# The end of the last feed-forward: roots cut into pieces, statistics from accumulators, norms and stores on ScalarE

## Chip, cores and metric

One core of one Trainium2 chip runs the whole program. The time is device time of one execution in microseconds (us), and less is better. A core has five engines with queues of their own, each in order: TensorE (PE, with its weight loads PEld), VectorE (DVE), ScalarE (ACT), GpSimd (POOL) and SyncE (SP), which here only issues DMAs. An instruction that waits holds up everything behind it on its engine.

## What is computed

A decoder of two layers with six sub-blocks (called A to F in the kernel), each followed by a layer norm of the residual sum. The activations are 4 batches of 512 rows by 512 columns, float32. The change touches the last sub-block only, a feed-forward with 4-bit weights, an RMS norm and the layer norm behind it:

```
def _L1_ffn_ref(x, gate_up_packed, gate_up_scales, down_packed, down_scales):
    ...
    gate_up = jnp.einsum('bsh,oh->bso', x, w_gu)
    gate, up = (gate_up[..., :I], gate_up[..., I:])      # I = 1408
    h = jax.nn.silu(gate) * up
    y = jnp.einsum('bsi,hi->bsh', h, w_down)
    rms = jnp.sqrt(jnp.mean(y * y, axis=-1, keepdims=True) + EPS)
    return y / rms
...
x = _layernorm(x + _L1_ffn_ref(x, ...), axis=-1)
```

with `_layernorm(x) = (x - mean) / sqrt(var + 1e-5)` over the 512 columns of a row.

## The kernel before

Every sub-block is a Python generator for one batch. `lanes` steps two of them in turn, so that the end of one batch is traced between the pieces of the next. The order of tasks is `E3 F0 F1 F2 F3` at the end, and a task may start when the one before it has said `"next"`. The framework's scheduler then orders the traced instructions on each engine and places the buffers and all waits; the order in the built program is therefore not quite the order of the source. `tc.issue_after(ins)` ties the instructions of a block behind `ins` on the engine of `ins`, as an order of issue alone.

`l1_ffn(b)` is F for batch `b`. It loads four tiles x of 128 rows by 512 and transposes them (`fx`, split into the pair `fxh`, `fxl`). Then it goes over 11 blocks of 128 hidden columns, each with `u` = 0 (gate) and 1 (up), and each of these over four groups `g` of 128 inputs, since every group has a scale of its own. One such piece is two matmuls into a PSUM bank `fg` (L1063), and `scaled` empties the bank: ScalarE writes g = 0 with its scale (L1021) and the gate's g = 3 into another tile (L1024), GpSimd adds that one (L1031), and VectorE adds the others to the running sum (L1027, called a scaled sum below; five of them in a block). Later follow Silu on ScalarE (L1035), the product on VectorE (L1039), the split into `fhh` on ScalarE (L1044) and `fhl` on GpSimd (L1045), and twelve matmuls into the four accumulators `facc` of the batch (L1054). A pass of the block has 28 matmuls: 16 of the pieces and 12 of the accumulators.

PSUM has eight banks in one pool. Four are held by the accumulators of a batch until its end. A next batch's pieces turn in the four that are left until its own accumulators start, so a bank that is freed late stops TensorE, whose queue is in order.

The end of a batch, called its tail, begins behind `yield "next"`: the residual x is loaded a second time; ScalarE squares the four accumulators with row sums (`fsq`, L1073); VectorE turns the sums into a mean square (L1076) and takes the inverse root for four columns at once: a shift (L158), a seed (L159), and three Newton steps of three operations (L161, L162, L163), all on 128x4. Then VectorE forms x + y/rms from PSUM (L1080), collects row statistics (`bn_stats` L168, `bn_aggr` L169), takes the second inverse root (L177, L158 to L163), and normalizes (L186). SP stores the four tiles (L189). The tails of F0, F1 and F2 lie beside the pieces of the next batch; the tail of F3 has nothing beside it.

```
        ss, ve = fm[:, 0:4], fm[:, 4:8]
        for i in range(NT):
            sq = self.t("fsq")
            nc.scalar.activation(sq, acc[i], AF.Square, accum_out=ss[:, i : i + 1])
```

Of the kernel before, what the change touches and what calls it, by code (L numbers as in the profile page):

```python
# [14 lines left out]
I32 = mybir.dt.int32  # L15
U8 = mybir.dt.uint8
AF = mybir.ActivationFunctionType
ALU = mybir.AluOpType
# [4 lines left out]
P = 128  # L23
NT = 4
MAGIC = 12582912.0
RSQRT_SEED = float(0x5F3759DF)
# [38 lines left out]
class Net:  # L65
# [88 lines left out]
    def rsqrt(self, ve, s):  # L154

        nc = self.nc
        sh, y, t = s[:, 0:4], s[:, 4:8], s[:, 8:12]
        nc.vector.tensor_scalar(sh.bitcast(I32), ve.bitcast(I32), 1, None, ALU.logical_shift_right)  # L158
        nc.vector.tensor_scalar(y.bitcast(I32), sh.bitcast(I32), -1.0, RSQRT_SEED, ALU.mult, ALU.add)  # L159
        for _ in range(3):  # L160
            nc.vector.tensor_tensor(t, y, y, ALU.mult)  # L161
            nc.vector.scalar_tensor_tensor(t, t, -0.5, ve, ALU.mult, ALU.mult)  # L162
            nc.vector.scalar_tensor_tensor(y, t, 1.5, y, ALU.add, ALU.mult)  # L163
        return y

    def ln_stats(self, y, i, ln):
        nc = self.nc
        nc.vector.bn_stats(ln[:, 8:14], y)  # L168
        nc.vector.bn_aggr(ln[:, 2 * i : 2 * i + 2], ln[:, 8:14])  # L169
# [835 lines left out]
    def l1_ffn(self, b):  # L1005
        nc = self.nc
        pipe = Pipe()
        x = self.load_x(5, b)
        yield
        yield  # L1010
        xT = []
        yield from self.feature_major(pipe, x, "fx", xT)
        yield from pipe.drain()
        acc, y, hs = [], {}, {}

        def scaled(i, u, g, ps):

            s = self.gs[:, (i * 2 + u) * 4 + g : (i * 2 + u) * 4 + g + 1]
            if g == 0:
                y[u] = self.t("fg")  # L1020
                nc.scalar.activation(y[u], ps, AF.Copy, scale=s)  # L1021
            elif g == 3 and u == 0:
                y2 = self.t("fg2")
                nc.scalar.activation(y2, ps, AF.Copy, scale=s)  # L1024
                y[u, 2] = y2
            else:
                nc.vector.scalar_tensor_tensor(y[u], ps, s, y[u], ALU.mult, ALU.add)  # L1027
            if g == 3:
                o = y.pop(u)
                if (u, 2) in y:  # L1030
                    nc.gpsimd.tensor_tensor(o, o, y.pop((u, 2)), ALU.add)  # L1031
                pipe.later(F_ACT, *((up, i, o) if u else (gate, o)))

        def gate(o):
            nc.scalar.activation(o, o, AF.Silu)  # L1035
            y["gate"] = o

        def up(i, o):
            nc.vector.tensor_tensor(o, o, y.pop("gate"), ALU.mult)  # L1039
            pipe.later(F_PAIR, pair, i, o)  # L1040

        def pair(i, o):
            hi, lo = self.t("fhh", F32R), self.t("fhl", F32R)
            nc.scalar.copy(hi, o)  # L1044
            nc.gpsimd.tensor_tensor(lo, o, hi.bitcast(F32), ALU.subtract)  # L1045
            for t in range(NT):
                pipe.later(F_DOWN + 2 * t, down, i, t, (hi, lo))

        def down(i, t, h):
            if len(acc) <= t:  # L1050
                acc.append(self.pb("facc"))
            c = slice(t * P, (t + 1) * P)
            for n, (l, r) in enumerate(((0, 0), (0, 1), (1, 0))):
                nc.tensor.matmul(acc[t], h[l][:, c], self.dn[i][r], start=i == 0 and n == 0, stop=i == 10 and n == 2)  # L1054

        for i in range(11):
            self.need("F", lambda: len(self.dn) > min(10, i + 1))
            for u in range(2):
                for g in range(4):
                    pipe.tick()  # L1060
                    ps = self.pa("fg")
                    for n in range(2):
                        nc.tensor.matmul(ps, self.gu[i, u][:, g * P : (g + 1) * P], xT[g][n], start=n == 0, stop=n == 1)  # L1063
                    pipe.later(F_SCALED, scaled, i, u, g, ps)
                    yield
        yield "next"
        x = self.load_x(5, b)
        yield from pipe.drain()
        fm = self.s("fm", 24, 2)
# [4 lines that stand above are left out]
            if i % 2:  # L1074
                yield
        nc.vector.tensor_scalar(ve, ss, 1.0 / 512.0, 1e-6, ALU.mult, ALU.add)  # L1076
        r = self.rsqrt(ve, fm[:, 8:20])
        ln = self.ln_tile()
        for i in range(NT):
            nc.vector.scalar_tensor_tensor(x[i], acc[i], r[:, i : i + 1], x[i], ALU.mult, ALU.add)  # L1080
            self.ln_stats(x[i], i, ln)
            if i % 2:
                yield
        self.finish(pipe, x, ln, 5, b)
        yield from pipe.drain()

    def need(self, key, ready):

# [119 lines left out]
```

## Time and profile before

| | |
|---|---|
| three runs | 1684.18, 1685.69 (median), 1687.63 us |
| the profiled execution | 1684.66 us, span 1682.9 us from its first to its last instruction |
| mean granted TensorE clock | 0.974 |
| TensorE busy | 1557.8 us, 93% of the span |
| VectorE busy | 1286.9 us, 76% |
| ScalarE busy | 1005.9 us, 60% |
| GpSimd busy | 675.3 us, 40% |
| scaled sums on VectorE (L1027) | 220, 162.3 us, 745 ns each |
| norms of all layer norms on VectorE (L186) | 96, 57.1 us |
| statistics of all layer norms on VectorE (L168) | 96, 66.0 us, 688 ns each |
| squares on ScalarE (L1073) | 16, 9.4 us, and 16 reads of the accumulator, 3.2 us |

In a timeline line the columns are the start, the duration, the engine, the line of the source, the operation, what it writes and reads with shapes, and how many of them follow each other; brackets hold the idle time before it and who ended it. In a line of the windows view the stretch is followed by its length, then busy time (and instructions) of PE, PEld, DVE, ACT and POOL, the granted clock, the DMA engines' busy share and GB/s. "L1027" is line 1027 of the kernel. The change inserts lines ahead of these, so that the scaled sum L1027 is L1043 in the changed kernel, the product L1039 is L1055, and the squares L1073 are L1089.

### The profile page before, as it was taken

Reading aid. Unit: us, or ns where it says so; the run is one execution under the profiler, and the core shown is the slowest. Engines: PE = TensorE matmul, PEld = TensorE weight load, DVE = VectorE, ACT = ScalarE, POOL = GpSimd, SP = SyncE. Lnnn points to the kernel's source line nnn. Section 1 sums busy time; section 2 is a strip of 40 time slices with the busy share of each in tenths; the row PEclk is TensorE's granted clock in tenths of the full one; section 3 lists DMA queues with packets and bytes.
Section 4 is the critical chain, followed back from the end, with each engine's and each line's share of the span. In section 5 each row is a group of like instructions: output and inputs, shape, how many; then the busy total and the mean of one; then the engine's idle time right before and its main releaser. Section 6 shows DMA issues by size and latency. Waiting matters only on the chain.

```text
span 1682.9 us, 25852 instructions
## 1 busy us (share of the span) xinstructions
PE 1557.8 (93%) x8246; PEld 1110.3 (66%) x8246; DVE 1286.9 (76%) x2804; ACT 1005.9 (60%) x2145; POOL 675.3 (40%) x672
## 2 busy tenths in 40 slices
PE   6899899999999989998999999999997889999995
PEld 4678687444454665466777767777676766786874
DVE  5787657999976668886565675756888999979795
ACT  4233243789877876876596864968624444444542
POOL 5574562555535401530344323353324345333332
PEclk8899999999999989999999999999999999999998
DMA  8572441454313742664441322423434632020000
GB/s 274 175 233 74 118 107 63 151 159 146 97 51 141 219 116 89 207 205 107 141 111 42 84 77 78 124 67 86 142 111 143 211 96 72 1 76 33 19 26 25
DMA packets 108359, 189.18 MB, mean 112 GB/s; under 512 B 17584, under 2 KB 19632, under 8 KB 108224
## 3 DMA queue, kind: packets, MB, share of 16 engines
q1 hardware_dynamic: 104096, 179.08, 34.9%
q0 software_dynamic: 4128, 8.46, 2.0%
q8 instruction: 65, 1.06, 0.3%
q14 instruction: 70, 0.57, 0.1%
HBM read 111.98 MB, written 41.94 MB: 91 GB/s over the span
## 4 chain that ended last, share of the span: by engine, by line
PE 49%; DVE 25%; ACT 9%; DMA 8%; issue 5%; POOL 2%; SPq 1%; DVEq 0%; ACTq 0%; POOLq 0%
PE fg L1063 6%; PE facc L1054 5%; DVE bsm L399 3%; PE dT L841 3%; DMA z<-had_scratch 2%; DVE fg L1027 2%; ACT de L831 2%; PE do L861 2%; PE pu L611 2%; DVE x L186 2%; PE dn L663 2%; PE pg L609 2%; PE dq L146 2%; PE dq L147 2%; PE dq L148 2%
## 5 line engine op out<-in xcount | busy, mean ns | idle before, releaser
L1027 DVE SCALAR_TENSOR_TENSOR fg<-fg,gs,fg 128x512 f32<-128x512 f32 x220 | 162.3, 745 | 36.8 <-PE fg L1063 17.8
L1063 PE MATMUL fg<-fxh,gu 128*128 128x512 f32 x352 | 144.0, 409 | 7.6 <-DVE fg L1027 4.6
L831 ACT ACTIVATE de<-de,dm 128x128 f32<-128x128 f32 (+3 forms) x256 | 143.0, 563 | 13.3 <-DVE dm L830 12.4
L830 DVE CUSTOM_DVE_ANT_0 de<-ds,negm,thr 128x128 f32<-128x128 f32 (+3 forms) x256 | 126.6, 546 | 31.1 <-PE ds L819 28.0
L407 POOL TENSOR_SCALAR be<-be,bsm 128x512 f32<-128x512 f32 x128 | 96.3, 765 | 117.1 <-DVE bsm L405 73.6
L1063 PE MATMUL fg<-fxl,gu 128*128 128x512 f32 x352 | 139.0, 395 | 0.0
L588 POOL TENSOR_TENSOR hl<-g,hh 128x512 fp32r<-128x512 f32 x64 | 84.0, 1320 | 115.7 <-ACT hh L587 96.1
L1031 POOL TENSOR_TENSOR fg<-fg,fg 128x512 f32<-128x512 f32 x44 | 61.1, 1388 | 128.5 <-ACT fg L1024 89.5
L401 ACT ACTIVATE be<-bs,bsm 128x512 f32<-128x512 f32 x128 | 87.6, 691 | 36.2 <-DVE bsm L399 30.3
L761 POOL TENSOR_TENSOR dql<-dqf,dqh 128x512 fp32r<-128x512 f32 x32 | 41.4, 1295 | 154.4 <-ACT dqh L760 120.8
L841 PE MATMUL dT<-ident,de 128*128 128x128 f32 x640 | 90.6, 279 | 7.9 <-ACT de L831 5.9
L1063 PEld LDWEIGHTS fg<-fxh,gu 128*128 128x128 f32 x352 | 66.9, 190 | 38.1 <-DVE fg L1027 14.3
L841 PEld LDWEIGHTS dT<-ident,de 128*128 128x128 f32 x640 | 72.2, 142 | 26.5 <-ACT de L831 13.4
L1021 ACT ACTIVATE fg<-fg,gs 128x512 f32<-128x512 f32 x88 | 60.4, 686 | 39.4 <-PE fg L1063 39.0
L399 DVE TENSOR_REDUCE bsm<-bs 128x1 f32<-128x512 f32 x128 | 83.9, 673 | 0.0
L677 PE MATMUL had<-had,z 128*128 128x128 f32 x512 | 74.2, 290 | 10.4 <-DMA z<-had_scratch 9.3
L1054 PE MATMUL facc<-p4h,fhh 128*128 128x512 f32 x176 | 71.6, 408 | 9.0 <-DVE fg L1027 6.2
L677 PEld LDWEIGHTS had<-had,z 128*128 128x128 f32 x512 | 68.0, 201 | 17.8 <-DMA z<-had_scratch 7.2
L423 PE MATMUL bo<-bpT,cT 128*64 128x512 f32 x256 | 75.7, 618 | 2.6 <-ACT bpT L414 1.5
L199 PEld LDWEIGHTS bT<-ident,be 128*128 128x128 f32 x512 | 54.8, 141 | 34.9 <-issue 11.8
L199 PE MATMUL bT<-ident,be 128*128 128x128 f32 x512 | 73.1, 281 | 4.7 <-POOL be L407 2.5
L135 ACT CAST qkh<-z 128x512 fp32r<-128x512 f32 x32 | 19.6, 620 | 94.4 <-POOL z L291 86.3
(329 smaller groups left out, 4759.8 us busy)
## 6 DMA issues: line engine op xcount, KB each, us to landing
x<-x SPq DMA_DIRECT2D x176, 256.0 KB, 3.1
had_scratch<-hw SPq DMA_DIRECT2D x64, 256.0 KB, 2.0
z<-had_scratch SPq DMA_DIRECT2D x64, 256.0 KB, 6.8
stk<-dqh SPq DMA_DIRECT2D x192, 64.0 KB, 2.0
tw<-in_wg_t SPq DMA_DIRECT2D x32, 256.0 KB, 4.5
sw<-z SPq DMA_DIRECT2D x64, 128.0 KB, 2.4
tw<-in_wu_t SPq DMA_DIRECT2D x32, 256.0 KB, 3.7
tw<-in_wd_t SPq DMA_DIRECT2D x32, 256.0 KB, 3.3
```

What stands on the lines that cost most here:

```text
L199: self.nc.tensor.transpose(pt[:, i * P : (i + 1) * P], srcs[i][:, j * P : (j + 1) * P], self.ident)
L399: nc.vector.tensor_reduce(sm[:, h : h + 1], ps, AX.X, ALU.max, negate=True)
L401: nc.scalar.activation(e, ps, AF.Exp, bias=sm[:, h : h + 1], accum_out=sm[:, 2 + h : 3 + h])
L407: nc.gpsimd.tensor_scalar(es[h][i], es[h][i], sm[:, 4 + h : 5 + h], 1.0, ALU.mult, ALU.mult)
L588: nc.gpsimd.tensor_tensor(lo, g, hi.bitcast(F32), ALU.subtract)
L677: nc.tensor.matmul(ps[:, c * P : (c + 1) * P], z[g * 4 + c][:, i * P : (i + 1) * P], self.had16, start=True, stop=True)
L830: nc.vector.tensor_tensor_reduce(es[i], ps, self.negm[:, 384 - P * i :], -1.0, self.thr[:, i : i + 1], ALU.add, ALU.min, n4[:, i : i + 1])
L831: nc.scalar.activation(es[i], es[i], AF.Exp, bias=n4[:, i : i + 1], scale=-1.0, accum_out=den[:, hh * 4 + i : hh * 4 + i + 1])
L841: nc.tensor.transpose(pt[:, o + (i - j) * P : o + (i - j + 1) * P], es[i][:, j * P : (j + 1) * P], self.ident)
L1027: nc.vector.scalar_tensor_tensor(y[u], ps, s, y[u], ALU.mult, ALU.add)
L1054: nc.tensor.matmul(acc[t], h[l][:, c], self.dn[i][r], start=i == 0 and n == 0, stop=i == 10 and n == 2)
L1063: nc.tensor.matmul(ps, self.gu[i, u][:, g * P : (g + 1) * P], xT[g][n], start=n == 0, stop=n == 1)
```

## The change

The inverse root can be issued in pieces: `rsqrt_spread` is a generator that issues shift and seed, and after a `yield` each one Newton step, every piece tied behind the scaled sum that was traced last (`self.summed`). Both roots of the tail use it. The row sums of the residual come from `accum_out` of the operation that forms it; GpSimd turns each into a negative mean; ScalarE squares x minus the mean with row sums. The norm becomes one ScalarE activation with a scale and a bias column, the bias from one GpSimd product, and ScalarE issues the stores. `finish`, which the other sub-blocks still use, is no longer called here.

```diff
+    def rsqrt_spread(self, ve, s):
+
+        nc = self.nc
+        sh, y, t = s[:, 0:4], s[:, 4:8], s[:, 8:12]
+        with self.tc.issue_after(self.summed.ins):
+            nc.vector.tensor_scalar(sh.bitcast(I32), ve.bitcast(I32), 1, None, ALU.logical_shift_right)
+            nc.vector.tensor_scalar(y.bitcast(I32), sh.bitcast(I32), -1.0, RSQRT_SEED, ALU.mult, ALU.add)
+        for _ in range(3):
+            yield
+            with self.tc.issue_after(self.summed.ins):
+                self.newton(ve, y, t)
...
-                nc.vector.scalar_tensor_tensor(y[u], ps, s, y[u], ALU.mult, ALU.add)
+                self.summed = nc.vector.scalar_tensor_tensor(y[u], ps, s, y[u], ALU.mult, ALU.add)
...
         nc.vector.tensor_scalar(ve, ss, 1.0 / 512.0, 1e-6, ALU.mult, ALU.add)
-        r = self.rsqrt(ve, fm[:, 8:20])
+        yield from self.rsqrt_spread(ve, fm[:, 8:20])
+        r = fm[:, 12:16]
         ln = self.ln_tile()
-        for i in range(NT):
-            nc.vector.scalar_tensor_tensor(x[i], acc[i], r[:, i : i + 1], x[i], ALU.mult, ALU.add)
-            self.ln_stats(x[i], i, ln)
+        tot, nmean, sq, nr = (ln[:, 4 * n : 4 * n + 4] for n in range(4))
+        for i in range(NT):
+
+            nc.vector.scalar_tensor_tensor(x[i], acc[i], r[:, i : i + 1], x[i], ALU.mult, ALU.add, accum_out=tot[:, i : i + 1])
+            nc.gpsimd.tensor_scalar(nmean[:, i : i + 1], tot[:, i : i + 1], -1.0 / 512.0, 1.0, ALU.mult, ALU.mult)
+            t = self.t("fsq")
+            nc.scalar.activation(t, x[i], AF.Square, bias=nmean[:, i : i + 1], accum_out=sq[:, i : i + 1])
             if i % 2:
                 yield
-        self.finish(pipe, x, ln, 5, b)
-        yield from pipe.drain()
+        v2 = ln[:, 16:20]
+        nc.vector.tensor_scalar(v2, sq, 1.0 / 512.0, 1e-5, ALU.mult, ALU.add)
+        yield from self.rsqrt_spread(v2, ln[:, 20:32])
+        r2 = ln[:, 24:28]
+        nc.gpsimd.tensor_tensor(nr, nmean, r2, ALU.mult)
+        yield
+        for i in range(NT):
+            nc.scalar.activation(x[i], x[i], AF.Identity, bias=nr[:, i : i + 1], scale=r2[:, i : i + 1])
+            nc.scalar.dma_start(self.xd[6][b, i * P : (i + 1) * P, :], x[i])
+            yield
```

In the changed kernel the residual is L1099, the means L1100, the squares L1102, the variance L1106, GpSimd's product L1109, the norms L1112 and the stores L1113; shift, seed and Newton steps are L175, L176 and L166 to L168; `fhl` is L1061.

More of the change, by code (lines that the diff above doesn't have):

```diff
@@ L160, in rsqrt, with newton @@
         for _ in range(3):
-            nc.vector.tensor_tensor(t, y, y, ALU.mult)
-            nc.vector.scalar_tensor_tensor(t, t, -0.5, ve, ALU.mult, ALU.mult)
-            nc.vector.scalar_tensor_tensor(y, t, 1.5, y, ALU.add, ALU.mult)
-        return y
+            self.newton(ve, y, t)
+        return y
+    def newton(self, ve, y, t):
+        nc = self.nc
+        nc.vector.tensor_tensor(t, y, y, ALU.mult)
+        nc.vector.scalar_tensor_tensor(t, t, -0.5, ve, ALU.mult, ALU.mult)
+        nc.vector.scalar_tensor_tensor(y, t, 1.5, y, ALU.add, ALU.mult)
+    def rsqrt_spread(self, ve, s):
+        nc = self.nc
+        sh, y, t = s[:, 0:4], s[:, 4:8], s[:, 8:12]
[5 more added lines that the diff above has]
+            with self.tc.issue_after(self.summed.ins):
+                self.newton(ve, y, t)
     def ln_stats(self, y, i, ln):
```

## The prediction

> **What bounds the kernel now.** I read the busy shares and the chain first, then the last 250 us, since the built order of the changed kernel is the same as before's on every engine up to the end of the first of the four batches of this phase. TensorE is busiest and carries half of the chain, VectorE a quarter:
>
> ```profile
> PE 1557.8 (93%) x8246; PEld 1110.3 (66%) x8246; DVE 1286.9 (76%) x2804; ACT 1005.9 (60%) x2145; POOL 675.3 (40%) x672
> PE 49%; DVE 25%; ACT 9%; DMA 8%; issue 5%; POOL 2%; SPq 1%; DVEq 0%; ACTq 0%; POOLq 0%
> ```
>
> The shares hide that each batch has two stages. The windows view, columns PE, PEld, DVE, ACT, POOL, clock, DMA, shows them for the third batch's end beside the fourth:
>
> ```profile
> 1598.00:1602.40 4.40, 2.38 (x10) 1.32 (x9) 4.26 (x8) 3.09 (x7) 2.52 (x2) 1.00 0.00 0
> 1602.40:1605.90 3.50, 3.50 (x9) 2.76 (x10) 2.23 (x5) 0.00 (x0) 0.00 (x0) 0.52 0.00 0
> 1616.00:1634.00 18.00, 16.93 (x71) 12.45 (x70) 17.80 (x34) 8.66 (x14) 8.66 (x6) 1.00 0.15 55
> 1634.00:1657.00 23.00, 23.00 (x103) 19.05 (x102) 16.89 (x24) 11.71 (x19) 10.05 (x8) 1.00 0.01 3
> ```
>
> From 1634 TensorE is full and VectorE has slack: TensorE bounds. In the tail VectorE is full (17.80 of 18.00), TensorE waits, and after the long wait its clock is 0.52. The timeline of TensorE has the two long waits:
>
> ```profile
> 1600.10 0.39 PE L1063 MATMUL fg<-fxl,gu 128*128 128x512 f32 x1
> 1602.38 0.68 PE L1054 MATMUL facc<-p4h,fhh 128*128 128x512 f32 x1 [1.90 <-DVE fg L1027]
> 1602.86 0.63 PE L1054 MATMUL facc<-p4l,fhh 128*128 128x512 f32 x1
> 1632.64 0.50 PE L1063 MATMUL fg<-fxh,gu 128*128 128x512 f32 x1 [0.99 <-DVE fg L1027]
> ```
>
> VectorE's timeline says why: two of the 128x4 operations took 1.2 us instead of 0.16, each ending with a GpSimd operation (1598.93 to 1600.22, 1600.18 to 1601.45), and the scaled sum that frees a PSUM bank stood behind them.
>
> ```profile
> 1599.07 1.17 DVE L159 TENSOR_SCALAR fm<-fm 128x4 int32<-128x4 int32 x1
> 1600.28 1.19 DVE L161 TENSOR_TENSOR fm<-fm 128x4 f32<-128x4 f32 x1
> 1601.50 0.16 DVE L162 SCALAR_TENSOR_TENSOR fm<-fm 128x4 f32<-128x4 f32 x1
> 1601.58 0.75 DVE L1027 SCALAR_TENSOR_TENSOR fg<-fg,gs,fg 128x512 f32<-128x512 f32 x1
> 1629.05 2.87 DVE L186 TENSOR_SCALAR x<-x,ln 128x512 f32<-128x512 f32 x4
> ```
>
> **What a tail costs now.** At full clock one matmul starts each 0.227 us. Start-to-start time above that, over the tail: 0.5 before the long wait, 2.05 in it (1600.10 to 1602.38 less one step), 1.7 at half clock (eight and a half steps of 0.43), 1.3 in small waits from 1606.2 to 1632, 1.3 at the four norms: 6.9 us. Three tails lie beside a next batch and are alike (long waits of 1.92, 1.92 and 1.90; at the norms 0.96, 1.00 and 0.99). The fourth has nothing beside it. So at best 20.7 us are to be had.
>
> **The change, walked through the same tail in its built order.** *First root.* Five of its operations still stand ahead of the first sum. The third (L176) meets the same GpSimd operation and ends at 1600.24. The second GpSimd operation, the next batch's fhl, now stands behind the four new GpSimd operations (L1100), and these wait for x, so nothing stalls the fourth. The first sum starts at 1600.56 instead of 1601.58, and TensorE's long wait falls from 2.05 to 1.0.
>
> *Second accumulator.* Then TensorE has seven matmuls, and the next needs the bank of the old batch's first accumulator, which the first L1099 frees (before, it went to a bank freed by a sum). On VectorE: sums at 1600.56, 1601.42, 1602.28 (0.855 apart when dependent, as 1601.58, 1602.43, 1603.29 before), the product to 1603.75, four root operations at 0.2, so L1099 at 1604.55, ended about 1605.4. TensorE ran out at 1603.2: a new wait of 2.2 us. A 1.9 us wait was followed by the halved clock and a 1.0 us one was not, so I move the halving here.
>
> *Statistics.* bn_stats, aggregation and four norms leave VectorE: 4 x 0.69, 4 x 0.17 and 2.87, 6.3 us. In their place it waits. Four L1099 at 0.66, the spacing of L1080, plus an accumulator read (none shown for this operation; a custom operation's takes 0.08, and I take 0 to 0.15, middle 0.08) end at 1607.6. The last GpSimd product of one column: the nearest row, a 128x1 tensor_scalar, is 0.29 (bounds 0.1 to 0.8, GpSimd spans being rough). The square: 0.6 plus a read of 0.2, as L1073. With handovers of 0.03 to 0.08 L1106 starts at 1608.83. All sums are queued behind L1106, though their matmuls are ready.
>
> *Second root.* In the built order eight operations (L1106 and seven of the root) stand in one block ahead of the next sum; only the last four lie between sums. ScalarE's fhh, now behind the four squares, ends at 1609.25, so GpSimd's fhl runs from 1609.33 to 1610.62 and the block's fourth operation meets it: 1.0 us more. The sum starts at 1611.34 and ends at 1612.09.
>
> *TensorE up to there.* The fourth accumulator waits for that sum's bank. Ahead of it stand 26 matmuls from the end of the first wait, at whatever clock. Before, 35 had started by 1612.1. Nine and a half less is 2.1 us. This holds the 1.0 gained, the 2.2, the halved clock and a last wait of about 1.3.
>
> *After it.* VectorE has no norms and few root operations left: I count one wait of 0.45 and ten restarts of 0.1 (1632.64 to 1632.97 is one step and 0.1), 1.45 us, where before 2.35 were still to come. So a tail costs 2.1 + 1.45 - 2.35 = 1.2 us more. A tenth for longer squares (a 128x512 activation from SBUF with a bias column is 0.72, not 0.6) makes 1.3, and three tails 3.9.
>
> *Stores.* Four norms (0.69 each) and four DMA issues move to ScalarE, in place of SP's queue, where nothing but loads was behind them. ScalarE's pieces of the next batch wait behind. TensorE then has some fourteen matmuls, 3.2 us, that need none of them. On SP four issues took 1.79 us:
>
> ```profile
> 1677.58 1.79 SPq L189 DMA_DIRECT2D out_dram<-x  x4
> ```
>
> No row shows one on ScalarE. From nothing to 0.45 each; at 0.45 the norms and issues are 4.2 us, and most is covered. I take nothing in the tails. The Trainium skill (Perfetto Trace Analysis, DMA Instruction, HWDGE) says that the sequencer is free only once the descriptors are made, which speaks against stores on ScalarE; by it each tail could lose the uncovered 1.0 us and the forecast would be 3 us later.
>
> *The last tail*, by the end of the timeline:
>
> ```profile
> 1666.10 0.17 DVE L1076 TENSOR_SCALAR fm<-fm 128x4 f32<-128x4 f32 x1 [7.14 <-ACT fsq L1073]
> 1674.62 0.17 DVE L177 TENSOR_SCALAR ln<-ln 128x4 f32<-128x4 f32 x1
> 1677.01 1.91 DVE L186 TENSOR_SCALAR x<-x,ln 128x512 f32<-128x512 f32 x4
> ```
>
> Unchanged to 1668.49, where the residual starts. Four L1099 end at 1671.5, the last square's read at 1672.7 (before, statistics to 1674.6), twelve operations at 0.2 to 1675.1, GpSimd's L1109 about 0.35, the ScalarE norms from 1675.5 at 0.58. The last issue starts at 1677.8 plus three issues of nothing to 0.45: 1677.8 to 1679.15. Before it was 1678.95. So 0.9 to 1.15 earlier at one end and 0.2 later at the other: I take 0.35 earlier.
>
> **Sum.** 3.9 - 0.35 = 3.55 us on the profiled execution of 1684.66 (span 1682.9). The median of the three runs is 1.03 above it: 1685.69 + 3.55 = 1689.2.
>
> On the clock the rows and the Trainium skill differ (TensorE: Matmul & The Clock Gate, What's actually happening: half rate after at least one idle window of about 3.4 us). By that rule waits of 1.0 and 2.2 us halve nothing. The sum would be the same, since VectorE sets when the 27th matmul starts.
>
> **The rivals.**
> *A wash.* The block misses the fhl (it needs L166 to start before 1609.33, and I have it at 1609.43). Then the sum comes 1.0 us earlier and a tail costs 0.3 more: 0.9 - 0.35 = 0.55 us, 1686.2; with a free accumulator read and the best last tail 1684.5. For it: 0.1 us decides. Against: the wait then moves to the operation after.
> *ScalarE's queue.* Issues of 0.45 are not covered, or GpSimd's small operations take 0.8: 1.8 us more a tail, 3.1 x 3 + 0.2 = 9.5: 1695.2. For it: SP's row; against: fourteen matmuls of cover.
> *Faster.* The statistics chain is quick and meets no lock, so the sum behind the block ends by 1609.9 instead of 1612.1: 2.2 us, so each tail costs 0.9 less than before, and with the last tail 0.9 shorter 3.6 us are gained: 1682.1. It decides from the fourth accumulator's wait: gone, or there. For it: 6.3 us of VectorE work do go. Against: they go behind the place where TensorE loses.
> *Not as said.* "Between the sums" holds for seven of the 24 root operations of a batch only, in the built order; the forecast has that in it.
>
> **How the numbers follow.** About 0.2% (3.4 us) can be told from no change. The forecast has 0.5 and lies on that line: with the accumulator read and small operations at their other values a tail costs 0.9 to 2.2 more, 2 to 6.5 us in all, of which I put 0.37 above the line and 0.13 below. The wash has 0.23, ScalarE's queue 0.15, faster 0.12. Slower 0.52, same 0.36, faster 0.12. The range runs from 1683.5, between the wash's best end and the faster case, to 1696.0, just past the queue; it leaves out most of the faster case and a little above.
>
> **What would show it.** Right: in the fed tails a TensorE wait near 1.0 us released by L1043, one near 2.2 released by L1099, one of about 1 us or more at a facc released by L1043, and none at the norms; a 1.0 to 1.3 us L166; DVE busy less by about 25 us over the span. Period between batches (first fxl to first fxl, 1501.83 to 1580.41, 78.58 now) 79.9. Wrong: a period under 78.6, no wait on L1099, ScalarE pieces late behind L1113, or a last store issued more than 1 us from now's place.

## The result, and the profile after

| | before | changed |
|---|---|---|
| median of five runs each | 1685.69 us (1684.18 to 1688.01) | 1692.48 us (1689.01 to 1693.61) |
| ratio, 95% interval | | 1.0039 (1.0024 to 1.0054) |
| profiled execution, span | 1684.66, 1682.9 us | 1689.01, 1687.3 us |
| second batch's first fxl to the end | 1424.30: 258.6 us | 1424.99: 262.3 us |
| period, second to third, third to fourth fxl | 77.53, 78.58 us | 79.08, 80.04 us |
| last square's read (L1073 / L1089), start to the end | 17.04 us | 16.18 us |

The change made the kernel 0.39% slower. 1689.2 us was forecast; the measured time lies inside the range and on the side that had the larger chance. Of the 4.4 us between the two spans, 3 x 1.5 come from the tails, the last batch gives 0.9 back, and 0.7 lies before the first tail, where nothing was changed: in the eleven profiled executions of this study the first fxl starts anywhere between 1329.9 and 1338.6 us. So kernels are compared below by the stretch from the second batch's first fxl to the end. It holds all three tails with a batch beside them, and the last one; it is read from one execution of each kernel. The medians differ by 6.8 us, 2.4 more than the profiled executions; the changed kernel's profiled execution is the lowest of its five, and no trace shows where the others spent more.

The page of the changed kernel, busy shares and chain:

```profile
PE 1559.4 (92%) x8246; PEld 1107.2 (66%) x8246; DVE 1262.0 (75%) x2772; ACT 1028.6 (61%) x2193; POOL 675.6 (40%) x692
PE 52%; DVE 23%; ACT 9%; DMA 7%; issue 5%; POOL 3%; SPq 1%; DVEq 0%; ACTq 0%; POOLq 0%
```

VectorE does 24.9 us less, as forecast, and the program is longer. The windows view of the changed kernel for the stretches shown before and the one between them, each moved by the 3.7 us by which this tail starts later:

```profile
1606.10:1609.60 3.50, 1.85 (x7) 0.89 (x6) 3.33 (x12) 0.32 (x1) 0.19 (x1) 1.00 0.00 0
1609.60:1619.70 10.10, 8.42 (x32) 5.08 (x30) 8.55 (x23) 6.74 (x16) 4.61 (x7) 1.00 0.01 2
1619.70:1637.70 18.00, 17.60 (x76) 13.72 (x75) 12.31 (x19) 11.53 (x19) 7.56 (x6) 1.00 0.16 59
```

The middle one of before, which starts at 1605.90, read:

```profile
1605.90:1616.00 10.10, 10.10 (x45) 8.00 (x44) 10.02 (x23) 3.80 (x6) 2.59 (x2) 1.00 0.01 2
```

In the last stretch VectorE falls from 17.80 to 12.31 busy, and TensorE gains only 0.7 us there (16.93 to 17.60). Ahead of it TensorE is busy in 8.42 of 10.10 us, where it was busy in all of them before. Most of the work was taken away behind the place where TensorE waits. TensorE's timeline has the waits, each with who ended it:

```profile
1605.06 0.50 PE L1070 MATMUL facc<-p4h,fhh 128*128 128x512 f32 x1 [0.88 <-DVE fg L1043]
1609.03 0.50 PE L1070 MATMUL facc<-p4h,fhh 128*128 128x512 f32 x1 [1.52 <-DVE x L1099]
1612.78 0.50 PE L1070 MATMUL facc<-p4h,fhh 128*128 128x512 f32 x1 [0.78 <-ACT fhh L1060]
1615.65 0.50 PE L1070 MATMUL facc<-p4h,fhh 128*128 128x512 f32 x1 [0.52 <-DVE fg L1043]
1618.63 0.50 PE L1079 MATMUL fg<-fxh,gu 128*128 128x512 f32 x1 [0.38 <-DVE fg L1043]
1633.32 0.50 PE L1079 MATMUL fg<-fxh,gu 128*128 128x512 f32 x1 [0.40 <-ACT fg L1037]
```

The other two tails have the same six to within 0.06 us. Start-to-start time above 0.227 us a matmul is 8.4 us in this tail, against 6.9 before: 1.5 us a tail. VectorE's timeline shows the block in front of the sum that the fourth accumulator waits for (dots stand for lines left out):

```profile
1608.21 0.75 DVE L1099 SCALAR_TENSOR_TENSOR x<-facc,fm,x 128x512 f32<-128x512 f32 x1
1608.89 0.08 DVE L1099 DVE_READ_ACCUMULATOR x<-facc,fm,x 128x1 f32 x1
1608.89 0.75 DVE L1099 SCALAR_TENSOR_TENSOR x<-facc,fm,x 128x512 f32<-128x512 f32 x1
...
1612.25 0.17 DVE L1106 TENSOR_SCALAR ln<-ln 128x4 f32<-128x4 f32 x1 [1.27 <-ACT fsq L1102]
...
1612.86 1.26 DVE L166 TENSOR_TENSOR ln<-ln 128x4 f32<-128x4 f32 x1
...
1614.84 0.75 DVE L1043 SCALAR_TENSOR_TENSOR fg<-fg,gs,fg 128x512 f32<-128x512 f32 x1
```

ScalarE's timeline shows the norms and stores, and the pieces of the next batch behind them:

```profile
1619.54 1.52 ACT L1112 ACTIVATE x<-x,ln 128x512 f32<-128x512 f32 x2 [0.40 <-POOL ln L1109]
1620.39 1.05 ACTq L1113 DMA_DIRECT2D out_dram<-x  x2
1621.48 1.52 ACT L1112 ACTIVATE x<-x,ln 128x512 f32<-128x512 f32 x2 [0.42 <-ACT x L1112]
1622.33 1.05 ACTq L1113 DMA_DIRECT2D out_dram<-x  x2
1623.42 0.69 ACT L1040 ACTIVATE fg<-fg,gs 128x512 f32<-128x512 f32 x1 [0.42 <-ACT x L1112]
1624.01 0.68 ACT L1037 ACTIVATE fg<-fg,gs 128x512 f32<-128x512 f32 x1
```

A row of 1.05 us is not two issues of 0.52. The same timeline of a narrower stretch shows them apart, each 0.34 us long; the second waits for the end of the norm that it stores:

```profile
1620.26 0.81 ACT L1112 ACTIVATE x<-x,ln 128x512 f32<-128x512 f32 x1
1621.10 0.34 ACTq L1113 DMA_DIRECT2D out_dram<-x  x1
```

ScalarE's queue is held for 3.9 us by norms and issues together. L1037 starts the chain of scaled sums of a piece; at 1624.01 VectorE had already been idle for over two of 3.0 us.

### The profile page after: what moved, and what is told of

Same layout as the page of the kernel before. It is cut to its first block, busy times and chain, and to the rows that moved or that the text cites. A ratio compares the mean times of both kernels' runs of the same rounds, so it can differ in the third digit from the quotient of the medians.

```text
span 1687.3 us, 25926 instructions
## 1 busy us (share of the span) xinstructions
PE 1559.4 (92%) x8246; PEld 1107.2 (66%) x8246; DVE 1262.0 (75%) x2772; ACT 1028.6 (61%) x2193; POOL 675.6 (40%) x692
## 3 DMA queue, kind: packets, MB, share of 16 engines
q8 instruction: 65, 1.06, 0.3%
## 4 chain that ended last, share of the span: by engine, by line
PE 52%; DVE 23%; ACT 9%; DMA 7%; issue 5%; POOL 3%; SPq 1%; DVEq 0%; ACTq 0%; POOLq 0%
PE fg L1079 7%; PE facc L1070 5%; DVE bsm L415 3%; PE dT L857 3%; PE dn L679 2%; PE pu L627 2%; ACT de L847 2%; PE pg L625 2%; DVE fg L1043 2%; PE do L877 2%; DMA z<-had_scratch 2%; PE had L693 2%; PE dq L146 2%; PE dq L147 2%; PE dq L148 2%
## 5 line engine op out<-in xcount | busy, mean ns | idle before, releaser
L1043 DVE SCALAR_TENSOR_TENSOR fg<-fg,gs,fg 128x512 f32<-128x512 f32 x220 | 162.6, 747 | 54.4 <-ACT fg L1037 23.1
L1037 ACT ACTIVATE fg<-fg,gs 128x512 f32<-128x512 f32 x88 | 60.3, 685 | 29.0 <-PE fg L1079 28.7
```

Of the source, the lines that this page charges most:

```text
L1043: self.summed = nc.vector.scalar_tensor_tensor(y[u], ps, s, y[u], ALU.mult, ALU.add)
```

## The experiments

The theory: the next batch's sums stand behind the statistics and the second root, and this sets the loss. The rivals: ScalarE's queue; or the norms. "Stretch" is the second batch's first fxl to the end, from the profiled execution; the ratio is to the kernel before, with its 95% interval. The two measures differ by up to 0.2% of the time (a_vn: 0.9 us more stretch than before, 4.4 us by its ratio), so the price of a wait is read from traces and whether a kernel is faster from the ratio.

| kernel | stretch us | ratio |
|---|---|---|
| before | 258.6 | |
| changed | 262.3 | 1.0039 (1.0024 to 1.0054) |
| a_sp: stores on SP | 262.0 | 1.0035 (1.0022 to 1.0048) |
| a_vn: norms on VectorE, stores on SP | 259.5 | 1.0026 (1.0014 to 1.0039) |
| a_bn: before, norms on ScalarE | 260.1 | 1.0013 (1.0002 to 1.0024) |
| a_late: second root later | 258.2 | 1.0008 (0.9998 to 1.0018) |
| b_onepiece: roots in one piece | 266.1 | 1.0043 (1.0026 to 1.0060) |
| b_late_vn: a_late and a_vn | 254.1 | 0.9984 (0.9973 to 0.9994) |
| b_early: b_late_vn, first root in another order | 257.9 | 0.9998 (0.9986 to 1.0010) |
| b_early_old: before, that order | 256.2 | 1.0000 (0.9986 to 1.0014) |
| c_product: b_late_vn, product behind L1099 | 253.1 | 0.9961 (0.9945 to 0.9977) |

**a_sp.**

```diff
-            nc.scalar.dma_start(self.xd[6][b, i * P : (i + 1) * P, :], x[i])
+            nc.sync.dma_start(self.xd[6][b, i * P : (i + 1) * P, :], x[i])
```

> The changed kernel with its four stores back on SP's queue; norms and statistics as changed. In the changed kernel's trace a batch's four norms and four issues hold ScalarE for 3.9 us (1619.54 to 1623.42) where four norms alone are about 2.4, and one TensorE wait of 0.4 us, released by ScalarE's late L1037, stands behind them. Theory (the sums of the next batch stand behind the statistics chain and the second root): the period between batches falls from 80.04 by at most 0.5 us, to 79.5 or more, the 0.9, 1.5 and 0.5 us TensorE waits stay, and the last tail gives another 0.3 to 0.9 us: 1.5 to 2.5 us off the changed kernel in all, still slower than before. Rival (ScalarE's queue): the period returns to 78.6 or less and the kernel stands level with before or under it.

The periods are 79.20 and 80.14, no shorter than the changed kernel's; the last tail is 0.6 us shorter (15.62 us from the last square's read to the end). Both are as expected of the theory, but its total is not: 0.2 us of stretch came back, not 1.5 to 2.5, and the four norms alone take 2.9 us, not 2.4. The issues on ScalarE cost nothing in the tails with a batch beside them, though ScalarE stands for 0.42 us at each pair, and 0.6 us at the end.

**a_vn.**

```diff
-            nc.scalar.activation(x[i], x[i], AF.Identity, bias=nr[:, i : i + 1], scale=r2[:, i : i + 1])
-            nc.scalar.dma_start(self.xd[6][b, i * P : (i + 1) * P, :], x[i])
+            nc.vector.tensor_scalar(x[i], x[i], r2[:, i : i + 1], nr[:, i : i + 1], ALU.mult, ALU.add)
+            nc.sync.dma_start(self.xd[6][b, i * P : (i + 1) * P, :], x[i])
```

> The changed kernel with the four norms on VectorE (multiply and add with the same two columns) and the stores on SP's queue: of the change only the statistics from accumulators and the roots in pieces are left. Theory: the costs in front of the norms (waits of 0.9, 1.5, 0.8 and 0.5 us) are all there, and a wait near 0.5 to 1.0 us comes back where VectorE does four norms in a row: period 80 to 80.7, time equal to the changed kernel or up to 2 us above it. Rival (norms and stores on ScalarE are what costs): period 78.6 or less.

Both were wrong: the periods are 78.43 and 79.40, 0.65 under the changed kernel's and 0.85 above before's. By the traces the norms on ScalarE cost 0.65 us a tail, and the statistics and the roots cost the rest; the times do not tell a_vn from a_sp or from the changed kernel (the intervals overlap). VectorE's timeline of this kernel shows why the norms are cheap here:

```profile
1619.90 1.90 DVE L1112 TENSOR_SCALAR x<-x,ln 128x512 f32<-128x512 f32 x4
```

Before, these four took 2.87 us, beside a GpSimd operation that began at 1628.60, and TensorE waited 0.99 behind them. Here they start 18.5 us after the last square (1601.40) instead of 31.5 (1597.53 to 1629.05), with no GpSimd operation beside them, and TensorE has no wait over 0.15 us from there to 1640.

This kernel also gave a look at the clock. TensorE's timeline and the windows view, third tail:

```profile
1609.19 0.77 PE L1070 MATMUL facc<-p4h,fhh 128*128 128x512 f32 x1 [1.52 <-DVE x L1099]
1611.47 0.63 PE L1079 MATMUL fg<-fxh,gu 128*128 128x512 f32 x1
1615.80 0.50 PE L1070 MATMUL facc<-p4h,fhh 128*128 128x512 f32 x1 [0.52 <-DVE fg L1043]
```

```profile
1605.90:1609.25 3.35, 1.71 (x7) 0.65 (x5) 3.14 (x12) 0.00 (x0) 0.02 (x1) 1.00 0.00 0
1609.25:1612.75 3.50, 3.50 (x9) 2.77 (x10) 2.20 (x8) 3.30 (x9) 0.74 (x4) 0.51 0.00 0
```

The same 1.52 us wait as in the changed kernel is followed by 3.4 us at half clock (a granted clock of 0.51 over 3.50 us), and the wait of 0.78 on fhh is gone in return. From the matmul at the 1.52 wait to the fourth accumulator it is 6.61 us, against 6.62 in the changed kernel at full clock (1609.03 to 1615.65). The half clock only fills time that TensorE would have waited.

**a_bn.**

```diff
-        self.finish(pipe, x, ln, 5, b)
-        yield from pipe.drain()
+        self.ln_rsqrt(ln)
+        nr = ln[:, 8:12]
+        nc.vector.scalar_tensor_tensor(nr, ln[:, 0:8].rearrange("p (i two) -> p i two", two=2)[:, :, 0], -1.0, ln[:, 24:28], ALU.mult, ALU.mult)
+        yield
+        for i in range(NT):
+            nc.scalar.activation(x[i], x[i], AF.Identity, bias=nr[:, i : i + 1], scale=ln[:, 24 + i : 25 + i])
+            nc.sync.dma_start(self.xd[6][b, i * P : (i + 1) * P, :], x[i])
+            yield
```

> The kernel before with only the norms moved to ScalarE (one more 128x4 operation for the bias column; stores on SP; bn_stats and roots as before). Theory: in before's trace the four norms on VectorE cost TensorE one wait of 1.0 us a tail, so this part by itself gains: period 77.6 to 78.3 against 78.58, 1 to 3 us less in all, and in the last tail four norms at 0.6 on ScalarE in place of 0.48 on VectorE give 0.5 back. Rival (ScalarE's queue): its L1021 come late behind the norms and a wait on ScalarE takes the place of the one on VectorE: period 78.6 or more, the time level with before or slower.

The rival was right: 77.59 and 79.20, and a last tail 0.5 us longer. ScalarE's and TensorE's timelines have the wait that came in place of the 0.99 us one:

```profile
1637.69 2.92 ACT L1089 ACTIVATE x<-x,ln 128x512 f32<-128x512 f32 x4
1640.52 0.60 ACT L1044 CAST fhh<-fg 128x512 fp32r<-128x512 f32 x1
1641.03 0.68 ACT L1021 ACTIVATE fg<-fg,gs 128x512 f32<-128x512 f32 x1
```

```profile
1641.76 0.50 PE L1063 MATMUL fg<-fxh,gu 128*128 128x512 f32 x1 [1.17 <-ACT fg L1021]
```

Four norms in a row stop the piece behind them on either engine, and a sum needs both.

**a_late.**

```diff
-        nc.vector.tensor_scalar(v2, sq, 1.0 / 512.0, 1e-5, ALU.mult, ALU.add)
+        yield
+        yield
+        yield
+        with self.tc.issue_after(self.summed.ins):
+            nc.vector.tensor_scalar(v2, sq, 1.0 / 512.0, 1e-5, ALU.mult, ALU.add)
```

> The changed kernel with the second root started three steps later and its first operation (L1106) ordered behind the latest scaled sum too: in the built order one sum stands right behind the four L1099, and one root operation between any two sums after it. Theory: the sum that started at 1614.84 starts about 1611, TensorE's 0.5 us wait at the fourth accumulator and the 0.4 us wait after it go, the waits of 0.9 and 1.5 us and the 0.8 us wait on fhh stay: period 78.5 to 79.2, the kernel 2.5 to 4.5 us under the changed one. Rival (ScalarE's queue, or the statistics themselves): period still 79.7 or more.

The theory was right: 4.1 us under the changed kernel, periods 77.45 and 79.20, the waits of 0.52 and 0.38 gone in all three tails (the second has a new one of 0.41 on fhl), and the ratio, 1.0008, clear of the changed kernel's interval. VectorE's timeline, right behind the four residuals:

```profile
1611.99 0.75 DVE L1043 SCALAR_TENSOR_TENSOR fg<-fg,gs,fg 128x512 f32<-128x512 f32 x1 [2.36 <-ACT fg L1037]
1612.66 0.16 DVE L1110 TENSOR_SCALAR ln<-ln 128x4 f32<-128x4 f32 x1
```

It starts 3.1 us after the last L1099, where it was 4.6 us in the changed kernel (1610.23 to 1614.84), and what holds it now is ScalarE: its L1037 stands behind the four squares and fhh.

**b_onepiece.** Both calls of `rsqrt_spread` replaced by `rsqrt`.

> The changed kernel with both roots in one piece, as before's helper has them (no steps in between, no order behind a sum); statistics, norms and stores as changed. In the built order all eleven operations of the first root, the four L1099, L1106 and six operations of the second root then stand in front of the next batch's first sum. Theory (the sums behind the statistics chain set the loss, and the pieces are what the change needs to bear it): the first long TensorE wait is released by an L1099 instead of a sum, about 1.2 us later, the sum comes at about the old place of 1614.8 or a little earlier, and a tail costs 0.5 to 2.5 us more than in the changed kernel, period 80.5 to 82.5. Rival (the pieces are what costs): period under 79.5.

As the theory had it: periods 80.59 and 81.19, the first long wait released by an L1099.

```profile
1606.64 0.50 PE L1079 MATMUL fg<-fxh,gu 128*128 128x512 f32 x1 [2.31 <-DVE x L1099]
1614.04 0.50 PE L1079 MATMUL fg<-fxh,gu 128*128 128x512 f32 x1 [1.83 <-DVE fg L1043]
1623.97 0.50 PE L1070 MATMUL facc<-p4h,fhh 128*128 128x512 f32 x1 [1.70 <-ACT fhh L1060]
```

So with the new statistics the pieces save 3.8 us of stretch; the ratios, 1.0043 and 1.0039, cannot tell the two kernels apart. With the old statistics and norms, the built order is the same on every engine with the pieces and without them, so that there they are nothing.

**b_late_vn.** The edits of a_late and a_vn together.

> The kernel with the late second root, and the four norms on VectorE with the stores on SP's queue. Theory: the two gains add up, since the late root took away the block in front of the sums (1.4 us a tail) and ScalarE's norms and issues held back its L1037 (0.65 us a tail): from the first batch's fxl to the end about 347.5 us, against 350.65 before, 354.28 in the changed kernel and 350.15 with the late root alone; time 0.1 to 0.3% under before. Rival (VectorE is full again, and the norms there make TensorE wait as before, 1 us a tail): no better than the late root alone, 350 or more.

The theory was right: 346.1 us from the first fxl, and faster than before. The two edits take 8.2 us of stretch off the changed kernel, more than the 6.8 that the two by themselves add up to. With VectorE unblocked the norms there cost nothing, and the last tail is 15.3 us.

**b_early.** On top of b_late_vn:

```diff
+                with self.tc.issue_after(self.freed.ins) if self.freed else ExitStack():
+                    self.summed = nc.vector.scalar_tensor_tensor(y[u], ps, s, y[u], ALU.mult, ALU.add)
...
-        yield from self.rsqrt_spread(ve, fm[:, 8:20])
+        nc.vector.tensor_scalar(fm[:, 8:12].bitcast(I32), ve.bitcast(I32), 1, None, ALU.logical_shift_right)
+        nc.vector.tensor_scalar(fm[:, 12:16].bitcast(I32), fm[:, 8:12].bitcast(I32), -1.0, RSQRT_SEED, ALU.mult, ALU.add)
+        yield
+        yield
+        yield
+        yield
+        with self.tc.issue_after(self.summed.ins):
+            self.newton(ve, fm[:, 12:16], fm[:, 16:20])
+        self.newton(ve, fm[:, 12:16], fm[:, 16:20])
+        self.newton(ve, fm[:, 12:16], fm[:, 16:20])
...
-            nc.vector.scalar_tensor_tensor(x[i], acc[i], r[:, i : i + 1], x[i], ALU.mult, ALU.add, accum_out=tot[:, i : i + 1])
+            res = nc.vector.scalar_tensor_tensor(x[i], acc[i], r[:, i : i + 1], x[i], ALU.mult, ALU.add, accum_out=tot[:, i : i + 1])
+            if i == 0:
+                self.freed = res
```

> As the kernel before in this list, with the first root in another order: three operations, one scaled sum, the other nine in one piece, two L1099, and only then the next sum. Theory: the first L1099 ends about 1.8 us earlier, so the 1.5 us wait that it releases goes, and the half clock that followed it in some runs has nothing to follow; the tail loses 4.0 to 5.5 us instead of 6.9 before and 8.4 changed; from first fxl to end 342 to 346 us. Rival (VectorE's work is the bound of the tail, whatever its order): the loss comes back as waits on later sums, and the stretch is 347 us or more.

The rival was right on the stretch: 349.9 us from the first fxl. The first wait is half as long, and the first residual starts 7.7 us after the first square instead of 9.6. But with the sums behind the residuals TensorE has only three matmuls between the two waits instead of seven, so the wait for the residual is as long as before, and the half clock follows it in two of three tails (in the other it follows the third wait):

```profile
1603.39 0.50 PE L1072 MATMUL facc<-p4h,fhh 128*128 128x512 f32 x1 [0.48 <-DVE fg L1045]
1605.83 0.50 PE L1081 MATMUL fg<-fxh,gu 128*128 128x512 f32 x1 [1.48 <-DVE x L1110]
1628.12 0.50 PE L1081 MATMUL fg<-fxh,gu 128*128 128x512 f32 x1 [0.93 <-DVE fg L1045]
```

The third wait has another cause. The four norms in front of that sum meet two GpSimd operations (1623.81 to 1626.66) and take 3.87 us, against 1.90 in a_vn:

```profile
1623.54 3.87 DVE L1129 TENSOR_SCALAR x<-x,ln 128x512 f32<-128x512 f32 x4
```

**b_early_old.** The same edit on the kernel before.

> The kernel before, with only that order of the first root (three operations, one scaled sum, nine operations, two residuals, then the next sum); bn_stats, the norms on VectorE and the stores on SP as before. Theory (the loss of a tail is the order around the first root, not where the statistics are computed): the long wait of 1.9 us falls to 1.0 or less and the residual's banks come early, a tail loses 4 to 5.5 us instead of 6.9, the period falls from 78.58 to 76.5 to 77.6, and the time is 3 to 8 us under before. Rival: the sums pushed behind the residuals make a wait of their own, period 78.3 or more.

The first wait moved as the theory said (0.49 for 1.90, no half clock in any tail), but a tail still loses 6.1 us of the 6.9, more than the 4 to 5.5 expected: a wait of 0.82 for the first residual, smaller ones behind it (0.24, 0.28, 0.50) and restarts of 0.1 give most back. The period is 77.73, the stretch 2.4 us shorter, and the time cannot be told from before's. The order of the first root is not the whole loss.

**c_product.** On top of b_late_vn, with `self.freed` set at the first L1099 as above:

```diff
-            nc.vector.tensor_tensor(o, o, y.pop("gate"), ALU.mult)
+            with self.tc.issue_after(self.freed.ins) if self.freed else ExitStack():
+                nc.vector.tensor_tensor(o, o, y.pop("gate"), ALU.mult)
```

> The kernel with the late second root, norms on VectorE and stores on SP's queue, and one edge more: the next batch's product (L1055, 0.6 us) is ordered behind the first L1099, so that in the built order it stands behind all four L1099 instead of in front of them. Theory (the second long wait, 1.52 us, lasts until the first L1099 ends, and everything on VectorE in front of that counts): the wait falls to about 0.9 us, and with it the half clock that followed in that kernel (1.6 us) may go: 0.6 to 2.2 us a tail, from first fxl to end 339.5 to 344.5 us against 346.06. Rival (the product feeds fhh and the accumulators after, so a later product gives the gain back): 346 us or more, with a new wait on fhh.

The wait on L1099 fell by 0.6 as worked out, and no tail had the half clock; but fhh, which needs the product, is late.

```profile
1608.20 0.50 PE L1072 MATMUL facc<-p4h,fhh 128*128 128x512 f32 x1 [0.92 <-DVE x L1101]
1612.22 0.50 PE L1072 MATMUL facc<-p4h,fhh 128*128 128x512 f32 x1 [1.05 <-ACT fhh L1062]
```

The periods are 76.28 and 77.31, 0.35 us a tail less than b_late_vn, between the two theories: the wait moved as worked out, and nearly half of it came back. (Its period ahead of the tails was 93.33 us instead of the 92 of all others, so the stretch from the first fxl, which the expectation names, reads 346.4, about 345.0 without that; from the second it is 253.1.) Of all kernels here it has the lowest ratio, though its interval touches that of b_late_vn.

## Why the prediction was right, and where its sum was wrong

By the trace of the changed kernel (third tail; the other two agree):

*The first wait* was put at 1.0 us lost and is 1.04 to 1.06. The third root operation met GpSimd (1.17 us), the fourth did not.

*The second accumulator* waits for the first L1099, as forecast, which starts 3.96 us after the first sum (3.99 worked out). The wait is 1.52 instead of 2.2: TensorE came 0.6 us later, by restarts of 0.1 and 0.3 after the first wait that I had not counted there.

*The half clock* was moved behind this wait, 1.7 us. It is not there in the changed kernel. This step was wrong as stated, and it did not matter for the reason given in the prediction: VectorE sets when the fourth accumulator starts. That place is unmoved with half clock (6.61 us in a_vn) and without (6.62 in the changed kernel).

*Statistics.* L1106 starts 8.0 us after the first sum (8.27 worked out): the accumulator read is hidden (L1099 0.67 apart, L1080 0.66), GpSimd's column is 0.19, the square 0.71. L166 met the fhl: 1.26 us. The sum behind the block starts 10.59 us after the first sum; 10.78 was worked out. The wait of about 1.3 at the fourth accumulator came as two, 0.78 on fhh ahead of it and 0.52 at it, so the sign named for it, one wait of about 1 us or more released by L1043, did not show. Up to there the changed tail has lost 6.5 us, the tail before about 4.5 after as many matmuls: 2.0, against 2.1. a_late shows that this block is the cause: with the block out of the way 4.1 us of stretch come back.

*After it* is the term that was mis-sized. 1.45 us were to come, 1.9 came. I had the wait at the norms gone, and 0.9 us with it. But norms on ScalarE make TensorE wait for ScalarE: 0.40 at 1633.32 by L1037, 1.17 in a_bn. a_vn prices it, 0.65 a tail (a_sp has no wait of 0.40 and loses as much, 8.5 us, so part of it is in shorter waits), and a_bn shows that by itself this part of the change loses (1.4 us of stretch, 0.5 of it in the last tail) where I had it gain. So a tail costs 1.5, not 1.3.

*Stores.* The upper end of 0.45 was a misreading: in SP's row of 1.79 us the four issues are 0.33 to 0.40 us each and start as the norms end. On ScalarE an issue is 0.34 us, and what costs more is that the second of each pair waits for its norm in the same queue. Nothing in the fed tails was right (a_sp), and so was my doubt at the end: the last tail is 0.6 us longer for it. The Trainium skill (Perfetto Trace Analysis, DMA Instruction, HWDGE) has the sequencer held until the descriptors are made. The rows agree, since the third norm starts at 1621.48, behind the issue that ends at 1621.44; but the 3 us that this was to cost by that sentence are not in the tails.

*The last tail* is 0.9 us shorter; 0.35 was taken and 0.9 to 1.15 was the far end. VectorE's norms at 0.48 and SP's issues would have made it 1.65 (a_vn: 15.39).

So 3 x 1.5 - 0.9 = 3.6 us was found in the traces where 3.55 was forecast; that this is so close is luck, since two errors, 0.2 a tail and 0.5 at the end, nearly cancel. The medians say 6.8; what they hold beyond the traced 4.4 stays open.

The rivals: *the wash* needed L166 to miss the fhl, and it met it in all three tails. *ScalarE's queue* was right that norms and issues hold ScalarE (3.9 us) and that L1037 comes late, and wrong in the length of an issue (0.34 us) and in the price: 0.65 a tail for norms and nothing for the issues, not 1.8. *Faster* fell at its own point, the wait at the fourth accumulator; a faster kernel came when the block was taken away and the norms were back on VectorE (b_late_vn). *Not as said* was true of the built order and false in worth: 3.8 us of stretch by b_onepiece.

## What to carry to other kernels

Work taken off a busy engine is worth what it frees at the place where the bound engine waits; here 25 us left VectorE, and TensorE lost 1.5 us a tail, since a chain over three engines had been put in front of the sums that free its banks. In an in-order queue, place the first operation of a chain behind the next consumers of its engine and not only its later pieces; that edit was worth 4 us of stretch. Before moving a run of operations to an idle engine, look which pieces of the other stream stand behind it there.

## What the runs showed of the hardware

The same TensorE wait, 0.9 and then 1.52 us with seven matmuls between, was followed by half clock in 5 of 15 tails (changed 0 of 3, a_sp 1, a_vn 2, a_late 1, b_late_vn 1); the 1.9 us wait in 6 of 6 (before, a_bn), and waits of 0.9, 0.9 and 1.05 in none of 3. A stretch at half clock in these tails lasts 3.41 us by the granted clock, once 6.83 (b_onepiece, behind a wait of 2.31). The Trainium skill (TensorE: Matmul & The Clock Gate, What's actually happening) has a free-running window of 3413 ns, which the lengths and the chance agree with; but it has the half rate come after an idle window, and in a_vn TensorE was busy in 1.71 of the 3.35 us ahead, so here the measurement decides.

Four accumulating operations on VectorE with reads of 0.08 us follow each other as closely as four without (0.67 and 0.66 us apart). A store's DMA issue took 0.34 us on ScalarE (median of 16) and 0.33 to 0.44 us on SP (a_vn); rows of several are longer because each waits for its norm.
